# A conditioned two-part block: the first pair's x loaded ahead of w2, rows with their own statistics, sums and transposes in other places

## The chip, the cores and the metric

The kernel runs on one core of a Trainium2 chip. A core has five engines that run side by side, each in the order of its own instructions: TensorE (PE; its weight loads are shown apart as PEld), VectorE (DVE), ScalarE (ACT), GpSimd (POOL) and SyncE (SP). SP, ACT and POOL also issue DMAs, each on a queue of its own, and all of these use the same 16 DMA engines. The metric is the device time of one execution in microseconds (us); lower is better.

## The reference, cut to what matters

x is (32, 128, 512) in f32, 32 batches of 128 tokens; `t` is a condition vector for each batch; `m` is true for masked tokens only, a tail of 0 to 32 tokens of each batch.

```python
shift, scale, gate_msa = split(silu(t) @ ada_w + ada_b, 3)
norm = where(m, layernorm(x) * (1 + scale) + shift, 0)
fwd  = gelu(norm @ ssm_w1 + ssm_b1) @ ssm_w2 + ssm_b2
bwd  = gelu(norm @ bwd_w1 + bwd_b1) @ bwd_w2 + bwd_b2   # the two flips cancel
x    = x + gate_msa * where(m, fwd + bwd, 0)
shift, scale, gate_mlp = split(silu(t) @ ffada_w + ffada_b, 3)
h    = gelu_tanh((layernorm(x) * (1 + scale) + shift) @ ff_w1 + ff_b1)
out  = x + gate_mlp * (h @ ff_w2 + ff_b2)
```

The first half changes masked tokens alone; the second half, a feed-forward block with a hidden size of 1024, runs over all tokens.

## The kernel before

**First half: slots.** The masked tokens are packed into 512 slots, four tiles of 128 (tile 0 to 3). From the mask the kernel computes which token stands in each slot (`find_slots`) and gathers its row of x into `xc` by indirect DMA on POOL (`gather_slots`). Each slot tile is normalised (`statistics`, `modulated`): bn_stats and bn_aggr on VectorE, EPS added, a power of -0.5 on POOL, then two VectorE instructions with the scale and shift rows of each slot, which small matmuls (`slot_part`) put into PSUM. `transposed_slots` transposes a tile on PE, and ACT copies it. `hidden` computes eight blocks of 128 hidden features for 256 slots at once (w1 holds ssm_w1 and bwd_w1 side by side, w2 the second layers, one above the other), `project` the second layer; `finish_slots` adds bias, gate and x and stores the tile in `x1_rows` in DRAM. Slot tiles 0 and 1 are finished first (L609 to L637), tiles 2 and 3 later (L1155 to L1200), mixed with the beginning of the second half.

**Second half: pairs.** NP = 4 pairs of eight batches, each pair two sides of four. `load_x` loads a pair's x, `take_first_half` overwrites the masked rows by indirect DMA from `x1_rows` (rows out of bounds are left as they are), then come statistics, normalisation, and the transpose to feature rows. For pair 0, side 0 is transposed in 32-column blocks by VectorE and by 16 small DMAs (`turned`), and `scaled` applies scale and shift on ACT; side 1 is transposed on PE (`transposed`), with scale and shift on VectorE. Both matmul layers are done as block products with sums and differences of quarters (`FirstProduct`, `SecondProduct`, one level of seven products inside another), for which VectorE forms sums of the weights in the opening: `Weights.combine` and `weight_sums(1)` to `(4)`; the latter are stored in DRAM (`t_rows`) and read back for every pair.

**Order.** From L361 on the order of each engine is that of the code: nothing is moved by a scheduler, and an instruction that waits holds all that stands behind it on its engine. PSUM has eight banks: two of tag "tr", three "h", three "o", given out in turn; a bank is free when its last reader is done.

**Around the change.** SP loads, in this order: `ada_w`, both halves of w1 and of w2 (behind a small POOL memset each, so that the gathers go first), `ff_w1`, `ffada_w`, bias rows, `ff_w2`, and last x of pair 0. VectorE, after slot tile 1: `slot_i` (L528), the gate rows of `mod1` (L529, in `modulation_rows`), then

```python
    every = ssm.tile([B, 2, P], BF16, name="every")     # L531
    nc.vector.memset(every, 1.0)
```

PE uses `every` in `count_more` (L589), which counts masked tokens for a loop at the end that runs when there are more than the slots hold; the call stands behind hidden blocks 0 to 2 of slot tiles 0 and 1, and the gate rows of tile 0 and the rows of tile 2 stand behind it:

```python
        h1 += hidden(xT_s, NH, w1, 0, AF.Gelu, "s0", ssm, range(4 * c, 4 * c + 3))
        if c == 0:
            total, start_at, more_i, col_l = count_more()
        gs.append(keep_gate(c, slot_part(c, 2, ps_o, "o")))
```

At L1137 and after, pair 0 takes its rows, its statistics are taken (`Statistics`, L706 to L712), side 0 is normalised before the hidden blocks of slot tiles 2 and 3 (L1155), and side 1 is transposed between the matmuls of the last `project` (L1193).

Of the kernel before, what the change touches and what calls it, by code (L numbers as in the profile page):

```python
# [9 lines left out]
F32 = mybir.dt.float32  # L10
# [12 lines left out]
def kernel(  # L23
# [90 lines left out]
    def broadcast_rows(t, vec, queue):  # L114

        n = vec.shape[0] // D
        each = t.shape[0] // n
        for j in range(n):
            queue.dma_start(
                t[j * each : (j + 1) * each, :],  # L120
                vec[ts(j, D)].rearrange("(o d) -> o d", o=1).to_broadcast([each, D]),
            )

    def load_ada(w, which, split):

        t = adap.tile([P, KC, 3 * D], F32, tag="ada", name=f"ada_{which}")
        for k in range(KC):
            nc.sync.dma_start(t[:, k, :split], w[ts(k, P), :split])
        return t
# [4 lines left out]
    def load_behind_gathers(t, w):  # L134
        nc.gpsimd.memset(t[0:1, 0, 0:1], 0.0)
        load_blocks(t, w)
# [25 lines left out]

    def group_of_tiles(name):
        return xnp.tile([P, G, D], F32, tag="xn", name=f"xn_{name}")
# [17 lines left out]
    def hidden(xT, n, w, bcol, func, name, pool, parts=range(HC)):  # L182

        h = []
        for f in parts:
            ph = ps_h.tile([P, 512], F32, tag="h", name=f"ph_{name}_{f}")
            for k in range(KC):
                nc.tensor.matmul(  # L188
                    ph[:, :n], w[:, k, ts(f, P)], xT[:, k, :], start=(k == 0), stop=(k == KC - 1)
                )  # L190
            t = pool.tile([P, n], F32, tag="h", name=f"h_{name}_{f}", bufs=HC)
            nc.scalar.activation(t, ph[:, :n], func, bias=biasT[:, bcol + f : bcol + f + 1])  # L192
            h.append(t)
        return h

    def project(i, h, w, name, between=None, bank=(ps_o, "o")):

        pool, tag = bank
        po = pool.tile([P, 512], F32, tag=tag, name=f"po_{name}_{i}")
        for f in range(HC):  # L200
            if between and f in between:
                between[f]()
            nc.tensor.matmul(po, h[f][:, ts(i, P)], w[:, f, :], start=(f == 0), stop=(f == HC - 1))  # L203
        return po

    def gated(po, bias, gate, name):

        t = tp.tile([P, D], F32, tag="t", name=f"t_{name}")
        nc.vector.tensor_tensor(t, po, bias, ALU.add)
        nc.vector.tensor_tensor(t, t, gate, ALU.mult)  # L210
        return t
# [36 lines left out]
    xc = []  # L248

    def find_slots(h, *bank):  # L250
        part = slice(h * NC // 2, (h + 1) * NC // 2)
        return tokens_of(pick[:, ts(h, NH)], slot_col[:, part], NC // 2, f"s{h}", ssm, *bank)

    def gather_slots(token_i):
        both = xp.tile([P, 2, D], F32, tag="x", name=f"xc_{len(xc)}")
        for c in range(NC // 2):
            gather(both[:, c], token_i[:, c : c + 1])
            xc.append(both[:, c])
# [29 lines left out]
    def slot_part(at, j, pool, tag):  # L288
        return of_slots(pick, at, mod1, j, pool, tag, f"part{j}_s{at}")
# [6 lines left out]
    def finish_slots(at, h1, gate):  # L296
        t = gated(project(at % (NC // 2), h1, w2, f"s{at}"), b2, gate, f"s_{at}")
        nc.vector.tensor_tensor(t, t, xc[at], ALU.add)
        nc.sync.dma_start(x1_rows[ts(at, P), :], t)
# [19 lines left out]
    def x_tile(b):  # L319
        return xp.tile([P, 2, D], F32, tag="x", name=f"x_{b}")  # L320
# [37 lines left out]
    x1_rows = dram.tile([NS, D], F32, name="x1_rows")  # L358
    opening = ExitStack()
# [63 lines left out]
    broadcast_rows(modb_a, ada_b, nc.gpsimd)  # L423
    half = const.tile([P, G], F32, name="half")
    nc.vector.memset(half, -0.5)

# [34 lines left out]
    nc.scalar.activation(s_sb, t_sb, AF.Silu)  # L461
    sT = ssm.tile([P, KC, B], F32, name="sT")
# [5 lines left out]
    nc.scalar.activation(warm, s_sb[0:1, 0:1], AF.Gelu)  # L468

    token_i = find_slots(0)  # L470
    gather_slots(token_i)

    load_behind_gathers(w1[:, :, :D], ssm_w1)
    load_behind_gathers(w1[:, :, D:], bwd_w1)
    load_behind_gathers(w2[:, :KC], ssm_w2)
    load_behind_gathers(w2[:, KC:], bwd_w2)
    for key, vec in (("ssm1", ssm_b1), ("bwd1", bwd_b1), ("ff1", ff_b1)):
        n = vec.shape[0] // P
        nc.gpsimd.dma_start(
            bias_rows[col[key] : col[key] + n, :], vec.rearrange("(c p) -> c p", p=P)  # L480
        )
# [12 lines left out]
    rows = [(slot_part(c, 1, ps_o, "o"), slot_part(c, 0, ps_h, "h")) for c in range(2)]  # L494
    pm = ps_o.tile([P, 512], F32, tag="o", name="pm_g")
    xT_s = ssm.tile([P, KC, NH], F32, tag="xT", name="xT_s0", bufs=2)
    xT_t = ssm.tile([P, KC, NH], F32, tag="xT", name="xT_s1", bufs=2)
    xn = group_of_tiles("s")
    mv, rstd = statistics(xc[:2], "s01")
    xn_s = [  # L500
        modulated(
            xc[c], *rows[c], f"s{c}", xn[:, c], (mv[:, c, 0:1], rstd[:, c : c + 1])
        )
        for c in range(2)
    ]
    modulation_matmuls(pm, ada_a, 2, 3, range(KC))
# [5 lines left out]
    ada_f = load_ada(ffada_w, "f", 3 * D)  # L512
# [4 lines left out]
    for t, vec in ((b2, ssm_b2), (b2b, bwd_b2), (modb_f, ffada_b), (fb2, ff_b2)):  # L517
        broadcast_rows(t, vec, nc.sync)
    nc.sync.dma_start(fw2, ff_w2.rearrange("(k p) f -> p k f", p=P))
    x_of = {0: load_x(0)}  # L520
    transposed_slots(xn_s[0], xT_s[:, :, ts(0, P)], "s0")
    transposed_slots(xn_s[1], xT_s[:, :, ts(1, P)], "s1")
# [6 lines left out]
    modulation_rows(pm, mod1, modb_a, 2, 3)  # L529

# [81 lines left out]
    for c in range(2):  # L612
        h1 += hidden(xT_s, NH, w1, 0, AF.Gelu, "s0", ssm, range(4 * c, 4 * c + 3))
        if c == 0:
            total, start_at, more_i, col_l = count_more()
        gs.append(keep_gate(c, slot_part(c, 2, ps_o, "o")))
        rows = slot_part(2 + c, 1, ps_o, "o"), slot_part(2 + c, 0, ps_o, "o")
        xn_s.append(modulated(xc[2 + c], *rows, f"s{2 + c}", xn[:, 2 + c]))
        if c == 0:
            Weights(fw1, KC // 2, FF // 2, t_1).combine(0, 1, 2, 3)  # L620
        h1 += hidden(xT_s, NH, w1, 0, AF.Gelu, "s0", ssm, range(4 * c + 3, 4 * c + 4))
        if c == 1:
            transposed_slots(xn_s[0], xT_t[:, :, ts(0, P)], "s2")
    weight_sums(1)
# [3 lines left out]
    weight_sums(2)  # L628
# [5 lines left out]
    fw2_of = Weights(fw2, HC // 2, D // 2, t_2)  # L634
    fw2_of.combine(0, 1)
    nc.vector.tensor_scalar(modb_f[B : 2 * B], modb_f[B : 2 * B], 1.0, None, ALU.add)
    finish_slots(1, h1, gs[1])  # L637

    store_weight_sums(3)
# [20 lines left out]

    fb2_step = const.tile([P, D // 2], F32, name="fb2_step")
# [5 lines left out]
    weight_sums(4)  # L667


    def take_first_half(p, xs, which=range(2 * G)):  # L670
        slots = NH if p == 0 else NS
        for i in which:
            b = 2 * p * G + i
            nc.gpsimd.indirect_dma_start(  # L674
                out=xs[i // G][i % G // 2][:, i % 2],
                out_offset=None,
                in_=x1_rows[:slots, :],
                in_offset=bass.IndirectOffsetOnAxis(ap=slot_i[:, b : b + 1], axis=0),
                bounds_check=slots - 1,
                oob_is_err=False,  # L680
            )
# [9 lines left out]
    ORDER = "P1U P5U P1V P5V P2U P6U P2V P6V P3U P7U P3V P7V P4U P4V".split()  # L691

# [45 lines left out]
    def turned(xn, xT, queues):  # L738

        R = 32  # L740
        src = xn.rearrange("p k i (q c) -> p q k i c", c=R)
        dst = xT.rearrange("p k (i b c) -> p b k i c", b=P // R, c=R)
        for b in range(P // R):
            for q in range(P // R):
                queues[b % len(queues)].dma_start(dst[ts(q, R), b], src[ts(b, R), q])  # L745
# [393 lines left out]
    stats = [Statistics(x_of[0][side], f"0_{side}") for side in range(2)]  # L1139
    xT = [new_xT(0, side) for side in range(2)]  # L1140
    for i in range(G):
        stats[0].one(i)
    stats[0].root()
# [8 lines left out]
    for i in range(G):  # L1152
        t = stats[0].normalised(i, xn[:, :, i])
        nc.vector.transpose(t, t)
    h1 = hidden(xT_t, NH, w1, 0, AF.Gelu, "s1", ssm)  # L1155
    turned(xn, xT[0], (nc.sync, nc.scalar))
# [3 lines left out]
    for i in range(G):  # L1160
        stats[1].one(i)
    stats[1].root()
    xn_b = []
    for c in range(2):
        both = ssm.tile([P, 2, D], F32, tag="xT", name=f"xn_0_1_{c}", bufs=2)
        for i in range(2):
            xn_b.append(stats[1].normalised(2 * c + i, both[:, i]))

    def turn(k):
        return lambda: transposed(1, xn_b, xT[1], k)  # L1170
# [14 lines left out]
    po_s2 = project(0, h1, w2, "s2")  # L1185

    def keep_and_turn():
        with_bias(2, po_s2)
        turn(2)()
        with_gate(2, gs[0])  # L1190
        with_x(2)

    between = {0: turn(0), 1: turn(1), 2: keep_and_turn, 4: turn(3)}  # L1193
    po = project(1, h1, w2, "s3", between, (ps_h, "h"))

    store_weight_sums(4, 2)
    of_x[0] = TokenBlocks(0, xT)
    of_x[0].one(1)
# [281 lines left out]
```

## Time and profile before

| | |
|---|---|
| median of three runs | 464.54 us (462.96 to 465.38) |
| span of the profiled execution | 463.6 us; no other time of it is given |
| granted PE clock, mean | 0.997 |
| first matmul of the hidden blocks | 20.93 us |
| end of `project` of slot tile 0 | 44.84 us |
| hidden blocks of slot tiles 2 and 3 | 58.10 to 71.94 us |
| first block product of pair 0 | 87.43 us |
| end of the last matmul | 458.9 us |
| DMA share in 5 to 50 us | 1.0 of the 16 engines |

The span runs from the first to the last instruction of the program. An engine is busy when an instruction runs on it; waits stand in square brackets, with what ended them. A matmul of f32 shows as two records[...]. Spans of PE are modelled at their ends, so starts are the safer times. A DMA's landing is counted from its issue.

### The profile page before, as it was taken

The page shows a single profiled execution, that of the slowest core. Times are in us where ns is not written, and L with a number is a line of the kernel's source. Part 1 is how long each engine was busy: PE and PEld are TensorE (multiplying, and loading weights), DVE is VectorE, ACT ScalarE, POOL GpSimd, SP SyncE. Part 2 cuts the span into 40 slices and gives each one's busy share as a digit, 9 for nine tenths or more (in the row PEclk, how much of TensorE's full clock was granted, in tenths as well). Part 3 has the DMA queues.
Part 4 walks back from the last instruction along what each step waited for, and adds up shares of the span by engine and source line. Part 5 has one row for each costly group of instructions (what it writes and reads, how often), then busy time and mean ns, then how long its engine had stood idle before and what let it go on. Part 6 is the DMA issues. An engine that isn't in the chain of part 4 may idle for free.

```text
span 463.6 us, 5827 instructions
## 1 busy us (share of the span) xinstructions
PE 448.9 (97%) x2000; PEld 364.4 (79%) x2000; DVE 330.6 (71%) x538; ACT 175.7 (38%) x380; POOL 159.8 (34%) x153
## 2 busy tenths in 40 slices
PE   6899999998999999999999999999999999999995
PEld 2475385676788888888888888888888887888884
DVE  4649778998669739996787498957963985433645
ACT  3122021743355271344455514454355144552000
POOL 6200082038981000489700005987000026560000
PEclk9999999999999999999999999999999999999998
DMA  8999836693206653923077259321872432213022
GB/s 280 386 408 364 322 107 95 219 326 104 85 5 211 97 102 105 354 90 113 1 229 113 68 169 310 99 81 34 212 105 60 155 142 79 81 74 109 0 81 105
DMA packets 82419, 70.42 MB, mean 152 GB/s; under 512 B 63168, under 2 KB 63696, under 8 KB 81362
## 3 DMA queue, kind: packets, MB, share of 16 engines
q1 hardware_dynamic: 67298, 57.03, 39.4%
q0 software_dynamic: 4480, 11.66, 7.2%
q10 hardware_dynamic: 10608, 1.32, 2.0%
q8 instruction: 17, 0.28, 0.3%
q14 instruction: 16, 0.13, 0.1%
HBM read 56.83 MB, written 13.17 MB: 151 GB/s over the span
## 4 chain that ended last, share of the span: by engine, by line
PE 72%; DVE 8%; DMA 5%; SPq 4%; POOL 4%; issue 3%; ACT 3%; POOLq 0%; ACTq 0%; DVEq 0%
PE a_o L1093 17%; PE a_m L906 14%; PE e_o L1093 13%; PE e_m L906 11%; PE ph_s L188 6%; PE po_s L203 6%; SPq L745 4%; DMA x<-in_x_dram 2%; POOL x L674 1%; DMA xc<-in_x_dram,token_i_s 1%; DMA tw<-t_rows 1%; ACT xT L728 1%; PE part_s L283 1%; POOL ha L957 1%; PE pm_f L263 1%
## 5 line engine op out<-in xcount | busy, mean ns | idle before, releaser
L957 POOL TENSOR_TENSOR ha<-p_m,ha 128x512 f32<-128x512 f32 x20 | 26.2, 1311 | 151.9 <-ACT ha L964 142.0
L1093 PE MATMUL e_o<-fw,ha 128*128 128x256 f32 x256 | 57.9, 379 | 0.0
L728 ACT ACTIVATE xT<-xT,modT 128x128 f32<-128x128 f32 x112 | 44.0, 480 | 31.9 <-DMA xT<-xn 31.9
L1093 PE MATMUL a_o<-t,hb 128*128 128x256 f32 x240 | 54.1, 379 | 0.0
L1093 PEld LDWEIGHTS e_o<-fw,ha 128*128 128x128 f32 x256 | 48.6, 190 | 6.6
L1093 PEld LDWEIGHTS a_o<-t,hb 128*128 128x128 f32 x240 | 45.6, 190 | 6.2
L674 POOL DMA_INDIRECT x<-x_rows,slot_i x32 | 38.1, 1192 | 30.1 <-DMA x_rows<-t_s 18.0
L868 ACT ACTIVATE hb<-hb,biasT 128x256 f32<-128x256 f32 x64 | 29.0, 500 | 29.1 <-POOL hb L990 19.3
L957 POOL TENSOR_TENSOR hb<-p_m,hb 128x512 f32<-128x512 f32 x20 | 29.3, 1464 | 18.9 <-DVE sx L835 18.6
L920 ACT COPY p_m<-e_m 128x512 f32<-128x512 f32 x27 | 15.8, 586 | 47.9 <-PE e_m L906 47.9
L964 ACT COPY ha<-e_m 128x512 f32<-128x512 f32 x32 | 18.5, 578 | 28.6 <-PE e_m L906 26.6
L931 DVE TENSOR_TENSOR e_m<-a_m,ha 128x512 f32<-128x512 f32 x20 | 14.0, 698 | 21.6 <-POOL ha L957 9.5
L188 PE MATMUL ph_s<-xT_s,w 128*128 128x256 f32 x128 | 28.6, 381 | 0.5 <-issue 0.5
L1093 PE MATMUL a_o<-t,s 128*128 128x256 f32 x128 | 28.9, 379 | 0.0
L1093 PE MATMUL a_o<-fw,ha 128*128 128x256 f32 x128 | 28.9, 379 | 0.0
L1093 PE MATMUL e_o<-fw,s 128*128 128x256 f32 x128 | 28.9, 379 | 0.0
L203 PE MATMUL po_s<-w,h_s 128*128 128x512 f32 x64 | 28.6, 592 | 0.0
L188 PEld LDWEIGHTS ph_s<-xT_s,w 128*128 128x128 f32 x128 | 24.0, 190 | 5.2 <-ACT h_s L192 1.5
L1093 PEld LDWEIGHTS a_o<-t,s 128*128 128x128 f32 x128 | 24.3, 190 | 3.3
L1093 PEld LDWEIGHTS e_o<-fw,s 128*128 128x128 f32 x128 | 24.3, 190 | 3.3
L1093 PEld LDWEIGHTS a_o<-fw,ha 128*128 128x128 f32 x128 | 24.3, 190 | 3.3
L868 ACT ACTIVATE ha<-e_m,biasT 128x256 f32<-128x256 f32 x48 | 20.1, 468 | 16.2 <-PE e_m L906 10.5
(210 smaller groups left out, 870.0 us busy)
## 6 DMA issues: line engine op xcount, KB each, us to landing
tw<-t_rows SPq DMA_DIRECT2D x16, 896.0 KB, 5.5
x<-in_x_dram SPq DMA_DIRECT2D x16, 512.0 KB, 6.8
gate<-gate_rows POOLq DMA_DIRECT2D x8, 1024.0 KB, 5.2
out_dram<-x SPq DMA_DIRECT2D x15, 512.0 KB, 3.3
xT<-xn SPq DMA_DIRECT2D x92, 64.0 KB, 2.4
fw<-in_L_cond_ff_w_dram SPq DMA_DIRECT2D x2, 2048.0 KB, 10.5
ada_f<-in_L_cond_ffada_w_dram SPq DMA_DIRECT2D x4, 768.0 KB, 16.7
ada_a<-in_L_cond_ada_w_dram SPq DMA_DIRECT2D x4, 512.0 KB, 6.7
```

The lines of the kernel that those rows point to most:

```text
L188: nc.tensor.matmul(ph[:, :n], w[:, k, ts(f, P)], xT[:, k, :], start=(k == 0), stop=(k == KC - 1))
L203: nc.tensor.matmul(po, h[f][:, ts(i, P)], w[:, f, :], start=(f == 0), stop=(f == HC - 1))
L674: nc.gpsimd.indirect_dma_start(out=xs[i // G][i % G // 2][:, i % 2], out_offset=None, in_=x1_rows[:slots, :], in_offset=bass.IndirectOffse ...
L728: nc.scalar.activation(out, src, AF.Identity, bias=shift, scale=scale)
L745: queues[b % len(queues)].dma_start(dst[ts(q, R), b], src[ts(b, R), q])
L868: nc.scalar.activation(dst[:, n], src[:, n], AF.Gelu_apprx_tanh, bias=biasT[:, f : f + 1])
L906: nc.tensor.matmul(bank[:, ts(n, QT)], self.w_block(j, product)[:, ts(n, P)], self.x_block(j, product), start=(product in ("P1", "P5") and ...
L920: nc.scalar.copy(p5, e)
L931: nc.vector.tensor_tensor(e, a, p5, add)
L957: nc.gpsimd.tensor_tensor(self.place(RESULT[j], c), self.p5[j], other, ALU.add)
L964: nc.scalar.copy(self.place(RESULT[j], c), src)
L1093: nc.tensor.matmul(part, src[:, k, ts(i, P)], w[product][:, k, :], start=(last and k == 0), stop=True, skip_group_check=True,)
```

## The change

What it does, in the order of the code:

- `own_statistics` computes mean and (variance + EPS)^-0.5 of each row and puts both in two columns behind the row's 512. It is used for x of pair 0 (tiles `raw`, 514 columns) and for slot tiles 0 and 1, which `finish_slots` now stores twice: 514 columns wide in `x1_wide` on SP, 512 wide in `x1_rows` on ACT. Pair 0's gathers read `x1_wide`, so a gathered row brings its statistics; the `Statistics` of pair 0 are gone.
- x of pair 0 is loaded on SP after w1 and before w2. w2 no longer waits for a POOL memset. Bias rows for `ada_b` and the first layers move from POOL to ACT. `b2` and `b2b` go ahead of `ffada_w`.
- Gate rows: the four matmuls of `pm_g` write four strips of 32 rows; ACT copies them, and one matmul with `strips` adds them up. The shift rows of slot tile 0 use an "o" bank.
- Slot tiles 0 and 1 each take their own statistics. Hidden blocks 0 to 2 of the first pair of slot tiles are done by halves of 128 slots.
- The statistics of `raw` stand after the gate rows of `mod1`; `every` and `count_more` keep their places in the code, now behind them.
- `combine` of `ff_w1`, `weight_sums` 1 to 3, their stores and `combine` of `ff_w2` stand in other places.
- Side 1 of pair 0 is normalised within the hidden blocks of slot tiles 2 and 3 and transposed from there on; the DMAs of `turned` are issued a quarter at a time behind hidden blocks 4 to 7.

```diff
+    def own_statistics(t, n, name):
+        for i in range(n):
+            st = stp.tile([P, 6], F32, tag="st", name=f"st_{name}_{i}")
+            row = t[:, i]
+            nc.vector.bn_stats(st, row[:, :D])
+            nc.vector.bn_aggr(row[:, D : D + 2], st)
+        var = t[:, :, D + 1]
+        nc.vector.tensor_scalar(var, var, EPS, None, ALU.add)
+        nc.gpsimd.tensor_tensor(var, var, half[:, :n], ALU.pow)
...
+        own_statistics(t, 1, f"s_{at}_x1")
+        nc.sync.dma_start(x1_wide[ts(at, P), :], t[:, 0])
+        nc.scalar.dma_start(x1_rows[ts(at, P), :], t[:, 0, :D])
...
-    broadcast_rows(modb_a, ada_b, nc.gpsimd)
+    strips = ssm.tile([P, B], F32, name="strips")
+    nc.vector.tensor_reduce(
+        strips, ident.rearrange("p (a b) -> p b a", b=B), axis=AX.X, op=ALU.add
+    )
...
+    broadcast_rows(modb_a, ada_b, nc.scalar)
...
-    load_behind_gathers(w2[:, :KC], ssm_w2)
-    load_behind_gathers(w2[:, KC:], bwd_w2)
...
+    raw = [x_tile(2 * n, 2) for n in range(2 * G // 2)]
+    for n, t in enumerate(raw):
+        nc.sync.dma_start(t[:, :, :D], x[2 * n : 2 * n + 2].rearrange("b s d -> s b d"))
+    load_blocks(w2[:, :KC], ssm_w2)
+    load_blocks(w2[:, KC:], bwd_w2)
...
+    for k in range(KC):
+        nc.tensor.matmul(
+            pm[ts(k, B), :], sT[:, k, :], ada_a[:, k, ts(2, D)], start=True, stop=True
+        )
+    nc.scalar.copy(gate_parts, pm)
...
-    mv, rstd = statistics(xc[:2], "s01")
+    xn_s = [modulated(xc[c], *rows[c], f"s{c}", xn[:, c]) for c in range(2)]
-    modulation_matmuls(pm, ada_a, 2, 3, range(KC))
...
+    def hidden_of_tile(f, c):
+        if c == 0:
+            ph_s[f] = ps_h.tile([P, 512], F32, tag="h", name=f"ph_s0_{f}")
+        for k in range(KC):
+            nc.tensor.matmul(
+                ph_s[f][:, ts(c, P)],
+                w1[:, k, ts(f, P)],
+                xT_s[:, k, ts(c, P)],
+                start=(c == 0 and k == 0),
+                stop=(k == KC - 1),
+                skip_group_check=True,
+            )
...
+    nc.tensor.matmul(pm[ts(2, B), :], strips, gate_parts, start=True, stop=True)
...
     modulation_rows(pm, mod1, modb_a, 2, 3)
+    for n, t in enumerate(raw):
+        own_statistics(t, 2, f"x_{n}")
+    for f in range(2):
+        hidden_of_tile(f, 0)
+    transposed_slots(xn_s[1], xT_s[:, :, ts(1, P)], "s1")
+    hidden_of_tile(2, 0)
 
     every = ssm.tile([B, 2, P], BF16, name="every")
...
-        if c == 0:
-            Weights(fw1, KC // 2, FF // 2, t_1).combine(0, 1, 2, 3)
...
-    weight_sums(1)
+    Weights(fw1, KC // 2, FF // 2, t_1).combine(0, 1, 2, 3)
...
-    weight_sums(2)
     finish_slots(0, h1, gs[0])
...
     weight_sums(3)
-    fw2_of = Weights(fw2, HC // 2, D // 2, t_2)
-    fw2_of.combine(0, 1)
+    store_weight_sums(3)
+    weight_sums(1)
...
+    weight_sums(2)
...
     weight_sums(4)
+    fw2_of = Weights(fw2, HC // 2, D // 2, t_2)
+    fw2_of.combine(0, 1)
...
-                in_=x1_rows[:slots, :],
+                in_=x1_rows if p else x1_wide,
...
-        t = stats[0].normalised(i, xn[:, :, i])
+        t = normalised(raw[i // 2][:, i % 2], xn[:, :, i])
         nc.vector.transpose(t, t)
...
+    after = {4 + b: [turn_rows(b)] for b in range(4)}
+    for f, g in ((6, normalised_of_side_1), (7, turn(0))):
+        after[f].append(g)
+    h1 = hidden(xT_t, NH, w1, 0, AF.Gelu, "s1", ssm, after=after)
...
-    between = {0: turn(0), 1: turn(1), 2: keep_and_turn, 4: turn(3)}
-    po = project(1, h1, w2, "s3", between, (ps_h, "h"))
+    po_s2 = project(0, h1, w2, "s2", {1: turn(1), 3: turn(2), 5: turn(3)})
...
+    po = project(1, h1, w2, "s3", bank=(ps_h, "h"))
```

## The prediction

> **What bounds the kernel now.** I read the page's first two parts first: they say which engine is full and where it is not.
>
> ```profile
> PE 448.9 (97%) x2000; PEld 364.4 (79%) x2000; DVE 330.6 (71%) x538; ACT 175.7 (38%) x380; POOL 159.8 (34%) x153
> PE   6899999998999999999999999999999999999995
> ```
>
> TensorE is busy for 448.9 of 463.6 us, so 14.7 us of idle time is all that better order can win, apart from removed matmuls. The view of PE's waits says where it lies (us, times, longest):
>
> ```profile
> PE pb L433 <- DVE mask_f L428: 3.3, 1, 3.3
> PE e_m L906 <- DVE e_m L931: 2.1, 3, 1.3
> PE e_m L906 <- DVE e_m L950: 1.9, 4, 0.8
> ```
>
> The first is the load of the mask, which stays; the others lie from 97 to 123 us (3.3 us together) and after 372 us (1.5 us). The end, 4.7 us after the last matmul, stays too. From 20.93 to 99 us PE doesn't wait at all: whatever delays it there is paid in full. So the opening decides. PE's timeline (start, duration, what):
>
> ```profile
> 12.86 1.99 PE L283 MATMUL part_s<-mod,pick 32*128 32x512 f32 x8 [0.15 <-DVE mod L273]
> 14.78 3.62 PE L263 MATMUL pm_g<-ada_a,sT 128*32 128x512 f32 x8
> 18.33 0.66 PE L179 MATMUL ptr_s<-ident,xn_s 128*128 128x128 f32 x4
> 19.55 0.66 PE L179 MATMUL ptr_s<-ident,xn_s 128*128 128x128 f32 x4 [0.56 <-DVE xn_s L172]
> 20.93 5.42 PE L188 MATMUL ph_s<-xT_s,w 128*128 128x256 f32 x24 [0.49 <-issue]
> 26.28 0.17 PE L589 MATMUL pt<-count,every 32*128 32x1 bf16 x1
> ```
>
> The reader is to see the small `pt` at 26.28: it needs `every`, which VectorE fills. VectorE's timeline says when it can:
>
> ```profile
> 21.16 0.69 DVE L273 TENSOR_TENSOR mod<-pm_g,modb_a 32x512 f32<-32x512 f32 x1
> 21.95 0.27 DVE L532 MEMSET every<- 32x256 bf16 x1
> 26.52 0.16 DVE L591 COPY totals<-pt 128x2 f32<-128x2 f32 x1 [4.29 <-PE pt L589]
> 72.29 0.65 DVE L706 BATCH_NORM_STATS2 st<-x 128x6 f32<-128x512 f32 x1
> 75.58 0.17 DVE L711 TENSOR_SCALAR ve<-mv 128x4 f32<-128x4 f32 x1
> ```
>
> `every` is ready 4 us before PE asks. From 72.29 to 75.58 four rows of statistics take 3.29 us, 0.82 us a row. Last, the landings of the four 1 MB halves of w1 and w2, issued by SP at 10.56, 11.05, 11.59 and 12.14 (last number: us from issue to landing):
>
> ```profile
> w<-in_L_cond_ssm_w_dram SPq DMA_DIRECT2D x1, 1024.0 KB, 7.0
> w<-in_L_cond_bwd_w_dram SPq DMA_DIRECT2D x1, 1024.0 KB, 10.6
> w<-in_L_cond_ssm_w_dram SPq DMA_DIRECT2D x1, 1024.0 KB, 12.7
> w<-in_L_cond_bwd_w_dram SPq DMA_DIRECT2D x1, 1024.0 KB, 14.8
> ```
>
> So they land at 17.6, 21.7, 24.3 and 26.9, one after the other, in a stretch where the DMA share is 1.0.
>
> **What the Trainium skill says.** (1) "DMA: Bandwidth & Descriptors", Queues, rings and completion order: each DMA engine consumes one issuer's descriptors in ring order. The landings above agree. (2) "TensorE: Matmul & The Clock Gate", The mechanism (Part 3): matmuls start and end in program order; only weight loads are pulled ahead. The timeline shows them in the order of the code, so a late `pt` holds all that follows. (3) The same page, What's actually happening (Part 1): PE's clock is halved after an idle window of about 3.4 us and comes back after a busy one. The trace agrees in kind: at the start `pm_ss` runs at half speed until about 10.5, and after the last matmul at 458.9 the granted clock falls within 2.1 us:
>
> ```profile
> L263 PE MATMUL pm_ss<-ada_a,sT x16: 592/1009/1062, 6.4 to 11.5; 128*32 128x512 f32 x16
> 461.00:463.60 2.60, 0.00 (x0) 0.00 (x0) 0.00 (x0) 0.00 (x0) 0.00 (x0) 0.52 0.06 19
> ```
>
> **The change part by part.**
>
> *Gate rows and first transposes.* `pm_g` goes from four matmuls in one column strip to four in four strips, then an ACT copy (0.59, L293's size) and one folding matmul. Strips run abreast: `pm_f` has 24 passes in 3.63 us, three abreast, 0.43 a step. So 0.86 + 0.86 replace 3.44: 1.7 us of PE saved. But the bank for `pm_g` was used by the scale rows of slot tile 0, read by VectorE until about 16.05 (statistics from 14.30, then 0.74), so it runs 16.1 to 17.0. The two slot tiles no longer share a root: one tile alone took 27.85 to 30.48, 2.63 us. POOL still issues two gathers until 16.39 ahead of the first root (0.55), so `xn_s` of tile 0 is ready at 17.85 (before 17.98), of tile 1 at 20.5 (before 19.50). PE: transposes 17.9 to 18.35 (0.44), fold 0.86, `ptr_b` 0.2, then hidden blocks by half tiles. Their 128-column passes aren't in the trace for w1; `pl_s` at 12.00 has such passes every 0.11, so one block of a half tile costs 8 x 0.11 = 0.9, against 1.73 for both halves before; bounds 0.9 and, if the weight load's 0.19 showed, 1.5. I take 0.9. Two blocks to 21.2, transposes 0.44, one block to 22.55, three more to 25.3. PE is at `pt` at 25.3, not 26.28: 1.0 us gained, with the old idle 0.56 and 0.49 filled.
>
> *x early, and its own statistics.* Four loads of 512 KB stand on SP between w1 and w2, so they take the places where w2 landed: 23.0, 24.3, 25.6, 26.9. The statistics of eight rows stand on VectorE after `mod` (now near 21.5) and before `every`. VectorE waits until 23.0, then needs 8 x 0.82 + 4 x 0.2 (the EPS addition, 16.04 to 16.11 and its start) = 7.4: it is through at 30.4, and the last tile's 26.9 + 1.84 doesn't bind. `every` 0.27, POOL's half of it 0.28 behind the roots: `pt` can start at 30.9. Queued behind it on PE is everything; VectorE's `totals` and slot tiles 2 and 3 wait too. PE stands from 25.3 to 30.9, 5.6 us; against before it is 30.9 - 26.3 = **4.6 us late**. This is a new wait where 4.3 us of VectorE's idle time seemed free.
>
> *The clock.* No stall like that is in the trace. A 5.6 us hole holds a whole window, or two mostly idle ones; the fall 2.1 us after the last matmul says that suffices. At the start PE was solid from 5.29 and slow to about 10.5: half of 5.2 is 2.6 us lost. Bounds: 0 if the clock stays, 3.4 if two windows pass. I take **2.5 us**.
>
> *w2, fw1, ada_f and biases.* All land 5.3 us later (2 MB at 1.0 MB per 2.65 us): w2 at 32.3, first used about 45; fw1, before 32.8, at 38.2, its sums now behind slot tile 3; ada_f (before 22.0 + 18.8 = 40.8; now behind b2) near 48, needed past 57. Nothing. The loads moved from POOL to ACT (ada_b, b1 biases) stand where ACT is idle, 3.4 to 4.9 and 6.7 to 19.0. Nothing; 1 us if ada_b came after 12.
>
> *Weight sums and the gather chain.* Let Q be the end of `po_s0` (before 44.84). VectorE then does bias, gate, x (to Q+2.6), own statistics 1.1, sums 3 and 1 (2.07 each), modb 0.42, slot tile 1 to Q+10.4, statistics 1.1, POOL's root 0.6: stored at Q+12.15. Store to first gather was 54.57 to 57.50: gathers begin at Q+15.05 (before Q+12.66). Eight gathers with the two stores took 57.5 to 65.8 and 67.4 to 72.5 (landed), 13.2 without the root between: Q+28.25; the last `normalised` 0.55: Q+28.9. PE asks for side 1 at the end of the hidden loop now, not after `po_s2`: Q+27.1 (71.94 - 44.84). Stall **1.8 us**; bounds 0 (quicker gathers) and 3 (the turning DMAs beside them). `scaled` on ACT ends near P1's start, as before. The statistics taken out of 61 to 76 hid behind 13.84 us of hidden matmuls: worth nothing.
>
> *Relief later.* The x1 and weight-sum stores start 2.3 us sooner against the first product, on queues full from 85.5 to 105, so the next pair's x may land sooner and POOL's gathers free VectorE earlier. Of the 3.3 us idle there I take **1.0** back; bounds 0 and 2.5.
>
> Sum: 4.6 + 2.5 + 1.8 - 1.0 = **+7.9 us**. The execution profiled spans 463.6, within the runs' 462.96 to 465.38 and 0.9 below their median, with nothing else of it given; I add to the median: 464.54 + 7.9 = 472.4.
>
> **The rivals.** *A, the forecast*, 472.4; own range 467.5 to 477; chance 0.70. *B, the same stall with little after it*: the clock stays up and relief is 2.5: 4.6 + 0 + 1.8 - 2.5 = +3.9, 468.4; chance 0.12. For it: the clock's threshold is seen once, at the end. *C, a pile-up*: clock 3.4, turn stall 3, w2 or stores late by 2, no relief: 4.6 + 3.4 + 3 + 2 = +13, 477.5; chance 0.06. *D, the other side*: the statistics stay hidden. That needs x's first tile by about 17.5, so that eight rows and `every` end by 25.3; it decides at that point. Then 1.0 gained, the turns unstalled, 2 of the 3.3 us won: -3, 461.5. Against it: x stands behind w1, which lands at 21.7. For it: VectorE's 4.3 and 2.4 us of idle time are there. Chance 0.12. That the statistics don't travel as meant doesn't change times.
>
> **How the numbers follow.** A's 467.5 to 477 leaves out B's lower part and C's upper part; with them the range is 466 to 477.5. What a measurement can tell from none is 0.5%, 2.3 us. Slower: A, B and C less the part of B within it, 0.84; same 0.05, from B and D; faster 0.11, from D.
>
> **What would show it.** In the changed trace: VectorE waiting for an x load after `mod`, then eight statistics in a row to about 30; PE's longest wait at the `pt` matmul, 4.9 to 6.2 us, released by POOL or VectorE; the hidden matmuls after it at double spacing for 3 to 7 us; a PE wait of 0.5 to 3 us at the first turn of side 1, released by VectorE; fewer waits from 97 to 123 us after P1. Wrong if `pt` waits under 2 us, if x lands before 20, or if PE's busy time grows by less than 1 us (then the clock held: 1.7 saved, 2.5 lost).

## The result, and the profile after

The changed kernel takes 478.15 us (median of four runs, 477.82 to 480.73) against 464.62 for the kernel before in the same session: 1.031 times as long, 95% interval 1.0274 to 1.0346. It is slower, as forecast, but by 13.5 us instead of 7.9; the time lies 0.65 us above the range. The profiled execution spans 476.3 us against 463.6. Of the six runs of e10 below (467.12 to 476.71 us) three count as slow runs and are left out of its time and ratio.

The page of the changed kernel, its parts on busy time and on slices of the span:

```profile
PE 452.7 (95%) x2026; PEld 368.0 (77%) x2026; DVE 335.0 (70%) x548; ACT 176.5 (37%) x381; POOL 159.1 (33%) x150
PE   6859997999899999999999999999999999999996
PEclk9879999899999999999999999999999999999999
```

PE is busy 3.8 us longer and idle 8.9 us longer. A slice is 11.9 us; the new dips and the lowered clock are all in the first eight slices, so the loss lies in the opening. The view of PE's waits (us in total, times, longest), with the rows that are new:

```profile
PE ptr L795 <- DVE xn L749: 4.4, 3, 2.3
PE pt L636 <- DVE every L579: 4.2, 1, 4.2
...
PE pm_g L522 <- DVE xn_s L182: 1.3, 1, 1.3
...
PE pt L636 <- POOL every L580: 0.6, 1, 0.6
```

Two of these the prediction named as waits (`pt`, the turns `ptr`). `pm_g` it had start at 16.1, behind its bank, but not as a wait with a price. PE's timeline at each place (start, duration, what, idle time before it):

```profile
16.20 1.93 PE L522 MATMUL pm_g<-ada_a,sT 128*32 128x512 f32 x8 [1.29 <-DVE xn_s L182]
...
30.87 0.18 PE L636 MATMUL pt<-count,every 32*128 32x1 bf16 x1 [4.21 <-DVE every L579]
31.62 0.18 PE L636 MATMUL pt<-count,every 32*128 32x1 bf16 x1 [0.57 <-POOL every L580]
31.62 2.10 PE L300 MATMUL part_s<-mod,pick 32*128 32x512 f32 x6
...
82.10 0.33 PE L795 MATMUL ptr<-ident,xn 128*128 128x128 f32 x1 [2.29 <-DVE xn L749]
```

VectorE's timeline shows what `pt` waits for: one wait for x, eight rows of statistics, and only then `every`:

```profile
23.22 0.69 DVE L168 BATCH_NORM_STATS2 st_x<-x 128x6 f32<-128x512 f32 x1 [1.45 <-DMA x<-in_x_dram]
...
30.39 0.17 DVE L171 TENSOR_SCALAR x<-x 128x2 f32<-128x2 f32 x1
30.54 0.27 DVE L579 MEMSET every<- 32x256 bf16 x1
```

And what the turns of side 1 wait for, rows of the gather that haven't landed:

```profile
81.49 0.55 DVE L749 TENSOR_SCALAR xn<-x 128x512 f32<-128x512 f32 x1 [2.80 <-DMA x<-x_wide,slot_i]
83.37 0.55 DVE L749 TENSOR_SCALAR xn<-x 128x512 f32<-128x512 f32 x1 [1.33 <-DMA x<-x_wide,slot_i]
84.25 0.55 DVE L749 TENSOR_SCALAR xn<-x 128x512 f32<-128x512 f32 x1 [0.34 <-DMA x<-x_wide,slot_i]
```

In the kernel before, the same turns run in one piece, without a wait:

```profile
78.65 0.60 PE L734 MATMUL ptr<-ident,xn 128*128 128x128 f32 x4
```

The clock, in windows of 2 us (stretch, length, busy time of PE, PEld, DVE, ACT and POOL with counts, granted PE clock, DMA share, GB/s):

```profile
30.00:32.00 2.00, 0.56 (x5) 0.48 (x8) 0.90 (x5) 0.00 (x0) 0.93 (x2) 0.50 1.05 396
34.00:36.00 2.00, 2.00 (x6) 1.55 (x6) 1.83 (x5) 0.32 (x1) 0.56 (x1) 0.50 1.02 410
80.00:82.00 2.00, 0.00 (x0) 0.00 (x0) 0.51 (x1) 0.52 (x2) 1.56 (x2) 1.00 1.08 146
86.00:88.00 2.00, 2.00 (x7) 1.35 (x6) 0.81 (x4) 1.49 (x2) 0.00 (x0) 0.53 0.92 136
```

After each of the two holes PE works at half speed. The trace's clock record gives three stretches at half speed: 16.2 to 19.6 us, behind the wait at `pm_g`, 29.8 to 36.7 and 84.5 to 87.9.

### The profile page after: what moved, and what is told of

It is laid out like the page before. It is cut to its first block, busy times and chain, and to the rows that moved or that the text cites. A ratio compares the mean times of both kernels' runs of the same rounds, so it can differ in the third digit from the quotient of the medians.

```text
span 476.3 us, 5888 instructions
## 1 busy us (share of the span) xinstructions
PE 452.7 (95%) x2026; PEld 368.0 (77%) x2026; DVE 335.0 (70%) x548; ACT 176.5 (37%) x381; POOL 159.1 (33%) x150
## 4 chain that ended last, share of the span: by engine, by line
PE 76%; POOL 3%; DVE 2%; issue 1%; DMA 1%; ACT 0%; POOLq 0%; DVEq 0%
PE a_o L1154 22%; PE e_o L1154 17%; PE a_m L967 17%; PE e_m L967 14%; PE po_s L216 3%; POOL x L726 2%; DMA x<-x_wide,slot_i 1%; PE a_m_alone L967 1%; PE last L1154 1%; POOL ha L1018 1%; PE ptr L795 0%; DVE e_m L992 0%; DVE s L906 0%; POOL ha L1047 0%; ACT p_m L981 0%
## 5 line engine op out<-in xcount | busy, mean ns | idle before, releaser
L726 POOL DMA_INDIRECT x<-x_rows,slot_i x24 | 29.0, 1210 | 10.3 <-issue 9.0
L199 PE MATMUL ph_s<-xT_s,w 128*128 128x256 f32 x104 | 24.6, 398 | 0.0
L967 PE MATMUL a_m<-xT,tw 128*128 128x256 f32 x96 | 24.6, 379 | 0.0
```

Source lines behind the costliest of these rows:

```text
L199: nc.tensor.matmul(ph[:, :n], w[:, k, ts(f, P)], xT[:, k, :], start=(k == 0), stop=(k == KC - 1))
L726: nc.gpsimd.indirect_dma_start(out=raw[i // 2][:, i % 2] if p == 0 else xs[i // G][i % G // 2][:, i % 2], out_offset=None, in_=x1_rows if ...
L967: nc.tensor.matmul(bank[:, ts(n, QT)], self.w_block(j, product)[:, ts(n, P)], self.x_block(j, product), start=(product in ("P1", "P5") and ...
```

## Where the time went, stretch by stretch

PE does the same work in the same order at three places in every kernel of this study: the first matmul of `pm_f`, the first block product of pair 0 (`a_m_alone`; 87.27 us in the kernel before by PE's timeline, while the chain of work that ends last picks it up at 87.43) and the end of the last matmul. The three stretches between them, from PE's timeline of one execution of each (us), with the times of the runs. A ratio is to runs of the kernel before in the same session, whose medians lie from 463.81 to 464.62:

| kernel | start to `pm_f` | `pm_f` to first product | first product to end | median (or one time) | ratio to before |
|---|---|---|---|---|---|
| before | 52.08 | 35.19 | 371.63 | 464.62 | |
| changed | 59.83 | 41.70 | 370.44 | 478.15 | 1.031 |
| e1_every_first | 51.86 | 42.73 | 370.44 | 470.25 | 1.0118 |
| e2_turns_back | 58.92 | 35.19 | 370.25 | 470.79 | 1.0143 |
| e3_both | 53.56 | 35.19 | 370.54 | 464.79 | 1.0012 |
| e4_clock | 56.83 | 42.58 | 370.26 | 475.59 | 1.0256 |
| e5_turned_later | 58.22 | 37.98 | 371.32 | 473.57 (one) | |
| e6_narrow_stores_later | 59.98 | 41.73 | 370.58 | 478.77 (one) | |
| e9_old_gate | 55.22 | 35.19 | 370.53 | 464.02 | 1.0005 |
| e10_x_early_alone | 53.34 | 39.29 | 371.58 | 470.80 | 1.0124 |
| e11_split_rows | 52.14 | 37.94 | 370.25 | 466.35 | 1.0039 |
| e12_early_moved_sums | 52.30 | 38.97 | 371.00 | 470.56 | 1.0153 |
| e13_split_rows_fold | 51.02 | 37.93 | 370.31 | 465.74 | 1.0052 |
| e14_sum_1_later | 52.23 | 36.52 | 371.73 | 465.09 | 1.0019 |

The changed kernel loses 7.75 us in the first stretch, 6.51 in the second and wins 1.19 in the third: 13.07 together. The experiments ask which part of the change made each.

## The experiments

All are edits of the changed kernel, but for e10 and e12, which start from the kernel before.

**e1_every_first: `every` ahead of the eight rows.** The fill of `every` and POOL's part of it move up; nothing else.

```diff
+    every = ssm.tile([B, 2, P], BF16, name="every")
+    nc.vector.memset(every, 1.0)
...
     for n, t in enumerate(raw):
         own_statistics(t, 2, f"x_{n}")
-    every = ssm.tile([B, 2, P], BF16, name="every")
-    nc.vector.memset(every, 1.0)
```

> Changed kernel with every filled ahead of the statistics of raw, nothing else moved. T1 (two waits of PE, each with a fall of its clock, make up the loss): the count matmul waits under 0.3 us instead of 4.8 and the clock doesn't fall there (2.4 us), so about 7.2 us less than the changed kernel, 471 us; the wait at the first turn of side 1 stays near 4.4 us. T2 (the chain of VectorE and the DMAs is later as a whole, and the waits only show it): most of it comes back at the next wait, slot tile 3's rows or the turn, and the time stays above 475 us.

470.25 us, ratio 1.0118 (1.0053 to 1.0182). The wait at `pt` is gone, the clock doesn't fall there, and the first stretch is 51.86 us, 7.97 shorter than in the changed kernel. (Some 1.1 us of that is because the clock didn't fall at 16 us in this execution: PE came to `pt` at 25.55, not 26.66.) The turns still wait 4.1 us:

```profile
PE ptr L795 <- DVE xn L749: 4.1, 3, 2.2
```

Behind them the clock is half for 6.8 us here (75.3 to 82.1) instead of 3.4, which makes the second stretch 1.0 longer.

So one 0.27 us instruction in the wrong place, behind 7.3 us of statistics, made the first loss and the half clock after it, some 7 us.

**e2_turns_back: the turns of side 1 back in the last `project`**, between the matmuls of slot tile 3, where the kernel before had them.

```diff
-    for f, g in ((6, normalised_of_side_1), (7, turn(0))):
-        after[f].append(g)
+    after[6].append(normalised_of_side_1)
...
-    po_s2 = project(0, h1, w2, "s2", {1: turn(1), 3: turn(2), 5: turn(3)})
+    po_s2 = project(0, h1, w2, "s2")
...
+    between = {0: turn(0), 1: turn(1), 2: keep_and_turn, 4: turn(3)}
+    po = project(1, h1, w2, "s3", between, (ps_h, "h"))
```

> Changed kernel with the four turns of side 1 back between the matmuls of slot tile 3's project, as before. T1: PE no longer waits 4.4 us for the last gathers, and the clock doesn't fall after it (1.7 us): about 6 us less than the changed kernel, 472 us; the count matmul's wait stays at 4.8 us. T2: the gather chain is later by more than the old place forgives, and a wait of 2 us or more is left at the turns: over 474 us.

470.79 us, ratio 1.0143 (1.008 to 1.0207). The second stretch is 35.19 us, to the digit that of before; `pt` still waits 2.67 and 0.58 us and the clock is half from 32.7 to 36.1. With side 1 asked for some 7 us later, the second loss is gone as a whole; what makes the gathers late is asked in e5.

**e3_both: the two together.**

> Both edits, every ahead of the statistics and the turns in their old place. T1: the two add up, 13 us less than the changed kernel, 465 us, no different from the kernel before by more than 1 us. T2: under 10 us of it comes back, over 468 us.

464.79 us, ratio 1.0012 (0.9993 to 1.0031): level with the kernel before. These two places explain the loss of 3.1% but for 0.1% (-0.1 to 0.3). What is left in the first stretch (53.56 against 52.08) goes with the waits at the gate rows and at the transposes behind them and the clock after these, half from 18.7 to 22.2:

```profile
16.19 1.06 PE L522 MATMUL pm_g<-ada_a,sT 128*32 128x512 f32 x8 [0.69 <-DVE xn_s L182]
18.39 0.83 PE L190 MATMUL ptr_s<-ident,xn_s 128*128 128x128 f32 x4 [1.14 <-DVE xn_s L183]
```

**e4_clock: the hole at `pt` filled.** Four extra matmuls (3.6 us of work whose result nobody reads) stand ahead of `pt`, so PE isn't idle while `every` is late.

```diff
+            for _ in range(4):
+                nc.tensor.matmul(spin, w1[:, 0, :P], w1[:, 0, :512], start=True, stop=True)
             total, start_at, more_i, col_l = count_more()
```

> Changed kernel with four more matmuls of 128x512 ahead of the count, whose result nothing reads: they fill 3.4 of the 4.2 us in which PE stands, and the wait itself is not shortened. If the halved clock costs what its record says (6.8 us at half, 5.0 of them busy), 2.4 us less than the changed kernel, 475.7 us, and the clock's record shows no half speed between 28 and 37 us. If the halved clock only fills time in which PE would wait anyway, no change, 478 us.

475.59 us, ratio 1.0256 (1.018 to 1.0333): by the medians 2.6 us less than the changed kernel, with more work, though the intervals of the two ratios overlap. `pt` starts at 31.03, as late as in the changed kernel, but the clock stays up, as the windows show:

```profile
30.00:32.00 2.00, 2.00 (x11) 0.53 (x9) 0.86 (x5) 0.00 (x0) 0.93 (x2) 1.00 1.05 399
32.00:34.00 2.00, 2.00 (x12) 1.67 (x10) 1.83 (x8) 0.59 (x1) 0.23 (x1) 1.00 1.03 411
```

The trace measures the price of the fall apart from the wait: from `part_s` behind `pt` to `pm_f` PE takes 25.77 us here, 25.79 in the kernel before and 28.20 in the changed one. The fall costs 2.4 us; the term of 2.5 was right. In e2, where the clock is half for 3.4 us and not 6.8, the same way takes 27.46, 1.7 more than before.

**e5_turned_later: who delays the gathers.** The 16 small DMAs of `turned` (64 KB each, pieces of 32 f32 numbers) go behind hidden block 8, and the last row of side 0 is normalised behind side 1.

```diff
-    after = {4 + b: [turn_rows(b)] for b in range(4)}
+    after = {6: [normalised_of_side_1, lambda: block_of_side_0(G - 1)],
+             7: [turn(0)] + [turn_rows(b) for b in range(4)]}
```

> Changed kernel with the last row of side 0 normalised behind side 1's rows, and the sixteen small DMAs of the turned blocks issued behind the eighth hidden block, so that they start when the gathers have landed. If these DMAs held the last gathers up (4.1 to 4.6 us from issue to landing against 2.1 to 2.7 before): the last three gathers land within 3 us and PE's wait at the first turn of side 1 falls from 4.4 to about 2.5 us. If the gathers are slow by their rows of 2056 bytes or the later start alone: the wait stays over 4 us. The time itself isn't the question, since the turned side comes later.

One run: 473.57 us. The turns wait 1.52, 0.49 and 0.13 us instead of 2.29, 1.55 and 0.56, and the clock doesn't fall after them; the second stretch is 3.7 us shorter. The DMA engines show why. The same stretch, full in the changed kernel (1.08 at 146 GB/s, above), is now nearly empty, and the last three rows come one behind another:

```profile
80.00:82.00 2.00, 1.38 (x5) 0.64 (x5) 1.97 (x4) 0.00 (x0) 0.00 (x0) 1.00 0.14 33
```

The last three gathers of this run land 2.5 us after their issue (median); in the changed kernel it is 4.1 (first this run, then the changed kernel):

```profile
x<-x_wide,slot_i POOLq DMA_INDIRECT x3, 2.5
x<-x_wide,slot_i POOLq DMA_INDIRECT x3, 4.1
```

So of the 4.4 us of waits, 2.3 go with the turned DMAs beside the gathers (the moved row of side 0 may have a small part in it). The 2.1 that stay fit the gathers' late start, which the prediction had priced at 1.8. The moved DMAs aren't free: a new wait of 0.79 us stands at 99 us.

**e6_narrow_stores_later: are the two stores of a slot tile in each other's way?** The 512-wide store moves from ACT to SP, behind the second 514-wide one.

```diff
-        nc.scalar.dma_start(x1_rows[ts(at, P), :], t[:, 0, :D])
...
+    for at in range(2):
+        nc.sync.dma_start(x1_rows[ts(at, P), :], wide[at][:, 0, :D])
```

> Changed kernel with the 512-wide stores of slot tiles 0 and 1 moved from ACT to SP behind the second 514-wide store. If the second store beside it made the wide store land 3.0 us after its issue (2.0 for the store before): it lands in about 2.0 us, the first gather starts about 1 us sooner after it, and PE's wait at the turn falls by up to 1 us. If the width of 2056 bytes does it: it still takes 3 us.

One run: 478.77 us, no gain. The first gather starts 3.58 us after POOL's power is done (64.83 to 68.41), 3.85 in the changed kernel. That settles little: the narrow stores now follow the wide one at once on the same queue, and the gather's release is put down to them. Neither the second store nor the width of the rows is shown to make the wait, and in e5, which leaves both as they are in the changed kernel, the same store landed after 2.65 us. The reason stays open.

**e9_old_gate: e3 with the gate rows of before** (four matmuls in one strip, no copy, no fold).

```diff
-    for k in range(KC):
-        nc.tensor.matmul(
-            pm[ts(k, B), :], sT[:, k, :], ada_a[:, k, ts(2, D)], start=True, stop=True
-        )
-    nc.scalar.copy(gate_parts, pm)
+    modulation_matmuls(pm, ada_a, 2, 3, range(KC))
```

> Both edits of the third experiment, and the gate rows as before: four matmuls one after the other in one strip, no copy on ACT, no folding matmul, shift rows of slot tile 0 in an h bank again. T3 (the strips saved nothing, because the long gate matmuls filled a wait for slot tile 0 that the short ones leave open, and the clock falls in that gap): PE doesn't wait between 14.8 and 18 us, the clock stays up from 10.5 us on, the count matmul starts near 25.5 us instead of 27.8, and the time is about 2 us under the third experiment, 462.7 us, under the kernel before. Rival (the strips' 1.7 us of PE is a real gain that something else ate): the time is 1 us or more over the third experiment.

464.02 us, ratio 1.0005 (0.9978 to 1.0032). The wait at the gate rows goes, and `pt` starts at 25.86, but the time is neither the 462.7 us of T3 nor 1 us over e3. In the profiled execution (467.03, slower than most of its 14 runs) a new loss follows: the eight rows stand ahead of slot tile 2 on VectorE, the banks for slot tile 3's rows come free late (their matmuls stretch over 3.01 us, 1.13 in the kernel before), and the clock is half from 37.8 to 41.2.

**e10_x_early_alone: the kernel before with x of pair 0 loaded between w1 and w2**, and nothing else of the change.

```diff
+    x_of = {0: load_x(0)}
     load_behind_gathers(w2[:, :KC], ssm_w2)
```

> Kernel before with nothing but the four loads of pair 0's x moved from behind the second layer's weights to between w1 and w2. T1: the later landings of w2, ff_w1 and ffada_w are hidden: within 1.5 us of the kernel before, with VectorE waiting some 5 us longer for ff_w1 and slot tile 3 done before PE asks. T2 (the DMA order is a cost by itself): 3 us or more over the kernel before.

Ratio 1.0124 (1.0044 to 1.0205): slower, as T2 said and T1 didn't allow for. The 2 MB of x push `ff_w1` back; VectorE, which sums it ahead of slot tile 3, waits for it, and PE waits for VectorE twice. VectorE's timeline, then PE's:

```profile
38.28 1.23 DVE L317 TENSOR_TENSOR t<-fw 128x1024 f32<-128x1024 f32 x1 [8.17 <-DMA fw<-in_L_cond_ff_w_dram]
```

```profile
61.18 0.87 PE L654 MATMUL ptr_mod<-ident,mod 96*128 96x96 f32 x4 [2.30 <-DVE mod L273]
```

So the early load on its own costs time. Whether the change's new places for the sums take that back is asked in e12.

**e11_split_rows: e9 with the eight rows split**, four behind slot tile 2 and four behind slot tile 3 on VectorE.

```diff
-    for n, t in enumerate(raw):
-        own_statistics(t, 2, f"x_{n}")
...
         xn_s.append(modulated(xc[2 + c], *rows, f"s{2 + c}", xn[:, 2 + c]))
+        for n in (2 * c, 2 * c + 1):
+            own_statistics(raw[n], 2, f"x_{n}")
```

> Built on e9_old_gate; the statistics of the eight early rows of x stand half behind slot tile 2 and half behind slot tile 3 on VectorE. T1 (each wait of the changed kernel comes from the place of one VectorE job, and nothing else in the change costs time): no PE wait over 0.3 us and full clock from 10.5 to 80 us; slot tile 3's rows take about 1.1 us instead of 3.01; first product at 86 to 87.3 (before: 87.27); 462.0 to 464.0 us, within 0.5% of the kernel before. T2 (something else in the change, such as the later weights or the stores beside the first product, costs 2 us or more): first product as under T1, but 466 us or more.

466.35 us, ratio 1.0039 (1.002 to 1.0058). The first stretch is as hoped for, 52.14. But now that PE comes in time, VectorE is late at `ptr_mod`, with the sums 3 and 1 (2.2 us each) ahead of slot tile 1, and the clock falls after it:

```profile
58.71 0.52 PE L692 MATMUL ptr_mod<-ident,mod 96*128 96x96 f32 x4 [1.02 <-DVE mod L290]
```

```profile
60.00:62.00 2.00, 2.00 (x6) 1.55 (x6) 2.00 (x4) 0.00 (x0) 0.00 (x0) 0.50 0.05 19
```

37.94 - 35.19 = 2.75 us: 1.02 of wait and 1.7 of half clock over 3.4 us. T1 had missed this place; T2's time was nearer, but the first product came at 90.08, where both had 86 to 87.3.

**e12_early_moved_sums: e10 with the sums where the change has them.**

```diff
-        if c == 0:
-            Weights(fw1, KC // 2, FF // 2, t_1).combine(0, 1, 2, 3)
...
-    weight_sums(1)
+    Weights(fw1, KC // 2, FF // 2, t_1).combine(0, 1, 2, 3)
...
     weight_sums(3)
+    weight_sums(1)
```

> Built on the kernel before: the first pair's x is loaded between w1 and w2, as in e10_x_early_alone, and the sums of fw1 and the other weight sums stand in the changed kernel's places; no mean or deviation travels with the rows. T1 (in e10 it was VectorE standing before the late fw1 that cost the time): VectorE's 8.17 us wait at fw1 shrinks below 3, PE's waits of 1.40 and 2.30 near 46 and 61 us vanish, first product at 87 to 88, 463 to 465.5 us. T2 (the early x costs by itself, since w2 and fw1 land 5 us later): first product later than 89, 467 us or more.

470.56 us, ratio 1.0153 (1.0122 to 1.0185). VectorE's wait at `ff_w1` shrinks from 8.17 to 0.65 us and the first stretch is 52.30, but `ptr_mod` waits 0.76 us, again with a half clock after it (59.0 to 62.4), and the second stretch is 3.8 us too long, part of which (1.3 us) has no wait above 0.13 beside it. The profiled execution (468.87) is the quickest of six. So T2's two numbers came out (first product at 91.27, 470.56 us). T1 was right about the waits of e10, which are gone, but the time hardly moved: another wait and a fall of the clock stand in their place, and part of the loss stays without a cause.

**e13_split_rows_fold: e11's split with the changed gate rows.**

> Built on e3_both (the changed kernel's gate rows with their fold stay); the eight rows' statistics split as in e11_split_rows. T1 (e3's remaining loss is the bank wait of the gate rows and the clock fall after it, ahead of the statistics): PE still waits about 0.7 us at the gate rows and 1.1 at the next transposes, clock half from 18.7 to 22.2, first product at 88 to 89, 463.5 to 465.5 us, no better than e3's 464.79 by more than 1. T2 (the statistics' place costs there too): first product before 87.5 and 462 to 463.5 us.

465.74 us, ratio 1.0052 (1.0031 to 1.0073). In its profile the gate rows wait 1.06 and the transposes 0.76 us, as in e3, but this time the clock stays up until 57.6, and `pt` starts at 25.22:

```profile
25.22 0.17 PE L634 MATMUL pt<-count,every 32*128 32x1 bf16 x1
```

That is the 25.3 of the prediction: the gain of 1.0 us in the opening is there (first stretch 51.02 against 52.08) where the clock holds. `ptr_mod` then waits 1.02 us, as in e11.

**e14_sum_1_later: e11 with sum 1 moved behind `ptr_mod`**, directly ahead of sum 2.

```diff
     store_weight_sums(3)
-    weight_sums(1)
...
+    weight_sums(1)
     weight_sums(2)
```

> Built on e11_split_rows; weight sum 1 moves on VectorE from ahead of slot tile 1 to directly ahead of weight sum 2. T1 (the 1.02 us wait at ptr_mod, and the half clock from 59.7 to 63.1 after it, come from the two sums of 2.2 us each that stand ahead of slot tile 1): both vanish, ptr_mod follows pm_f by 5.5 us as before instead of 6.57, the first product starts 35.2 us after pm_f, at 87.0 to 87.7, and the time falls by 2.7 us, to 462.5 to 464.0 us: even with the kernel before, or up to 1.5 us faster. T2 (the clock fell there for another reason, such as the short row matmuls alone): the wait goes but the clock still falls, the first product at 89 or later, 465 us or more.

465.09 us, ratio 1.0019 (1.0 to 1.0039). The wait at `ptr_mod` and the half clock after it both go: 52.23 to `pm_f`, and `ptr_mod` 5.48 us behind it, as before. The next late part is ACT, which issues half of the turned DMAs (about 1 us each) between the activations of the last hidden blocks:

```profile
79.16 1.13 PE L216 MATMUL po_s<-w,h_s 128*128 128x512 f32 x2 [1.05 <-ACT h_s L203]
```

In the profiled execution a wait of the feed-forward part was also longer (2.56 us from 115 us on, 1.25 in e11), and the clock was half from 117.7 to 121.1. The waits went as T1 said; the time (462.5 to 464.0) did not. No kernel of this study is faster than the kernel before.

## Why the prediction was right in kind and too small

By its own steps, with PE's starts before and after:

| step | predicted | measured |
|---|---|---|
| `pt` and what stands behind it | +4.6 | +5.33 (26.29 to 31.62) |
| half clock after it | +2.5 | 7.75 - 5.33 = +2.42 |
| w2, `ff_w1`, `ffada_w` later | 0 | 0 (hidden blocks of tiles 2 and 3: 57.94 to 65.69, still +7.75) |
| turns of side 1 | +1.8 | +6.51 (first product: 87.27 to 101.53, less 7.75) |
| relief after the first product | -1.0 | -1.19 |
| sum | +7.9 | +13.07 |

**The step that failed is the turn stall.** The mechanism was the one named, gathers that land after PE asks, released through VectorE; its size was wrong, and so was its upper bound of 3 us. The prediction counted the gathers' chain: late start, eight issues, one landing. That much is about 2.1 us, what e5 leaves with the turned DMAs out of the way. It named "the turning DMAs beside them" only as part of the bound. In the trace these were worth 2.3 us of wait, since the gathers' landing, taken as unchanged, went from 2.7 us (median before) to 4.1 for the last ones. And the stall was long enough for the clock to fall a second time (84.5 to 87.9), 1.7 us that stood in no term, although the same reasoning had been applied to `pt` and the 2.1 us at the program's end had been read as enough for a fall. 4.4 of waits, 1.7 of clock and 0.4 that no single wait shows make the 6.51. `turned` was moved into the gathers' window (its DMAs are issued from 78.2 to 85.5 us; before from 72.4 to 79.4, with the last gather landed at 72.5), and its cost was worked out for PE and VectorE, not for the queues. The first gather also began at Q + 15.9, not Q + 15.05: the 514-wide store landed 3.0 us after issue where the 512-wide one had taken 2.0. e6 moved the second store and won 0.3 us, so the reason stays open.

**`pt`** was right where it was worked out: `every` filled from 30.54 (said: 30.4), `pt` at 30.87 (said: 30.9). Two things around it were missed. First, the second of the two `pt` matmuls needs POOL's part of `every`, and POOL did the last power first (30.64 to 31.33), hence 0.57 us more; the prediction had put that part "behind the roots" and then not counted it. That is most of what 5.33 has over 4.6. Second, PE reached `pt` at 26.66, not 25.3, so that its wait was 4.21 us and not 4.9 or more: the clock was half from 16.2 to 19.6, behind the 1.29 us that the gate rows waited for their bank. The prediction had `pm_g` start at 16.1 all the same, but gave the gap no clock. This is hidden under the wait for `every` and shows only where that wait is removed, in e3. e13 shows the forecast gain of 1.0 us without the fall.

**The clock term** was taken from the slow 5.2 us at the start of the program and came out within 0.1 us; e4 shows the same 2.4. The size has luck in it: it depends on how long the clock stays down and how much of that time PE works, and with 3.4 us at half, in e2, it was 1.7.

**Relief** had the right size and the wrong place, so the size is luck. The waits from 97 to 123 us, where it was expected, sum to 3.26 us before and 3.43 after (111 to 137 us). Instead the waits of 0.29 at 373 and 0.40 at 401 us are gone; the other 0.5 isn't tied to a wait.

**The rivals.** B (the clock holds) falls with the clock record. C, the pile-up, has the nearest time. It took the turn stall (3) and the clock (3.4) higher, which was right, but counted 2 us on a late w2 or late stores, of which there is no sign, and on no relief, which came. D, statistics that stay hidden, decided at an x landing by 17.5; x landed at 23.2. e1 and e3 add that D's premise was narrower than it need be: the statistics may run late if `every` doesn't stand behind them.

## What to carry to other kernels

On an engine in program order, a new block of work must be checked against every small instruction behind it that another engine waits for: 0.27 us of `memset` behind 7.3 us of statistics cost some 7 us, and moving it up cost nothing that e1 shows. When a step is moved on the compute engines, redraw the DMA queues too, because a stage that is ready earlier brings its transfers into another's window. And price a stall on TensorE twice, once for the wait and once for the clock: in this opening 1.7 us for each 3.4 us at half clock in which PE has work, as often as the clock falls.

## What was not expected of the hardware

**Short waits can halve the clock.** The Trainium skill, "TensorE: Matmul & The Clock Gate", What's actually happening (Part 1), describes a free-running window of 3413 ns; the traces agree: every stretch at half clock that ends within a program lasts 3.4 or 6.8 us, and e13's full stretch from 9.8 to 57.6 us is 14 such windows. The same page's table Why this matters for your kernels asks only that gaps stay under some 3 us. Here a single wait of 0.76 us (e12), 1.02 (e11) or 1.29 (changed kernel, at 16 us) was followed by 3.4 us at half clock, while 1.25 us at 116 us in e11 was not, nor were 1.16 and 0.66 in e1's opening.

Counting the windows on from the edges in each trace's clock record tells more than single waits do. Where a window at full clock holds no matmul of 32 rows or 32 columns, it was followed by a fall in all 21 cases in which PE was idle for 2.14 us of it or more (the least is e11's, at its last matmul), and in none in which it was idle for 1.94 or less (the most is e14's). So about 2 us in one window were enough, not 3, as the prediction had read from the 2.1 us at the program's end. The windows with a fall after less idle time all hold matmuls of 32 rows (`part_s`): the idle time is 0.76 us in e12, 1.02 in e11 and 1.42 in the changed kernel at 16 us. e9's window from 34.4 to 37.8 us shows no wait of PE at all, but 2.6 us of `part_s`, and the clock fell. That fits matmuls of 32 rows counting for less, but no run varied them alone, so it is not shown, nor by how much. And as the window starts elsewhere in each execution, the same code can fall or not: the same opening gave 1.82 us of idle in one window in e3, with a fall, and 1.12 in e13, without.

**Small pieces fill the DMA engines.** "DMA: Bandwidth & Descriptors", Why small descriptors are slow (HBM only), says that transfers within SBUF don't suffer from them; its example is a remote transfer. Here `turned`, which moves 128-byte pieces from SBUF to SBUF, stands beside the gathers where the share is 1.08 at 146 GB/s, 0.98 of it in pieces under 512 bytes; the large loads reach 396 GB/s at 1.05. So here they do suffer, and the measurement decides: for the gathers beside it, this was a full queue.
